# Layer 2 into its feed-forward: norms of three batches as pieces of the attention, a fixed TensorE order up to the gathers, and layer 3's first keys loaded in two column parts

## The chip, the cores and the metric

The kernel runs on one core of a Trainium2 chip. The metric is the device time of one execution in microseconds; the number given for a kernel is the median of its runs. The engines are called PE (TensorE), DVE (VectorE), ACT (ScalarE), POOL (GpSimd) and SP (SyncE, which here issues DMAs).

## What is computed

Four layers run in one program over x of 4 batches x 256 tokens x 256 features, each as a norm, a cross attention to a context (4 x 1601 x 256) and a residual addition, then a norm, a feed-forward and a residual addition. The change lies at the end of layer 2's attention, in layer 2's feed-forward, and in the loads that open layer 3:

```python
x = x + _L2_xattn_ref(_layernorm(x, axis=-1), ctx_2048, ...)
x = x + _L2_ffn_ref(_layernorm(x, axis=-1), L2_ffn_Wr, L2_ffn_br, L2_ffn_Wg, L2_ffn_Wu, L2_ffn_Wd)
x = x + _L3_xattn_ref(_layernorm(x, axis=-1), ctx_2048, ...)

def _layernorm(x, axis=-1, eps=1e-05):
    m = jnp.mean(x, axis=axis, keepdims=True)
    v = jnp.var(x, axis=axis, keepdims=True)
    return (x - m) / jnp.sqrt(v + eps)

def _L2_ffn_ref(hidden_states, Wr, br, Wg, Wu, Wd):   # 4 experts, 1024 hidden units each, best one per token
    logits = x @ Wr + br
    probs = jax.nn.softmax(logits, axis=-1)
    top_w, top_idx = jax.lax.top_k(probs, 1)
    g = jnp.einsum('td,edf->tef', x, Wg); u = jnp.einsum('td,edf->tef', x, Wu)
    y = jnp.einsum('tef,efd->ted', jax.nn.silu(g) * u, Wd)
    ...
```

## The kernel before

The layers follow each other in one instruction stream per engine. A scheduler places the instructions of each engine, by their dependences and its own costs; an instruction given to `self.pin` keeps its place in the program's order relative to other pinned ones on its engine. While `self.strict` is true, `self.mm` and `self.ordered` pin every matmul that goes through them. In the kernel before, `strict` is false in layer 2's feed-forward. Register loads (`value_load`) are not pinned by it.

**Layer 2's attention** (`l2_xattn`) goes through units of one batch and one group of four heads, `units = [(b, g) ...]`, with four groups per batch. The loop over heads and column pairs (`step` 0 to 7) interleaves the scores of one head with the softmax, the turns of the probabilities (`pT`, DVE, L1613) and the value products of the head before; `pieces` prepares the next unit, and `project` multiplies by `wo` and adds to x (`acc`, L1635). The last unit's tail follows the loop.

**Layer 2's feed-forward** (`l2_ffn`) first takes the norm of each batch (`layernorm`, L1033: statistics on DVE, the root as a Sqrt activation on ACT in `rstd`, L125, which needs its own activation table, then a reciprocal and `f2xn` on DVE, L160), writes `f2xd` to memory, transposes on PE (`tp_ln`, L1040) into `f2xT`, with the copy by ACT (L114) or DVE (L112) in turn, and multiplies by the router (`f2lg`, 8 x 2 products of 4 columns). Batches 0 to 2 have their final x long before the attention's end, and the scheduler moves their statistics and Sqrt there, while the writing of `f2xn` stays behind the attention. From the logits DVE and ACT work out softmax, gate and one-hot choice `oh`; `f2ct` (two PE products) counts tokens per expert; DVE works out the place of each token (`te` to `cols`, L1077 to L1113) and the expert of each of the 11 token blocks (`ei`, L1128). `f2st` (8 products of `rows` and `cols`) gives `src`, by which POOL gathers the blocks (`f2xr`, L1134). Each block is transposed (`brought`, `f2tpx`, L1148), its expert's number is loaded into a register of each engine that uses it (L1150), and `gated`, `turned` and `down` go over 4 chunks x 11 blocks, with `load(c)` fetching the weights of a chunk.

**Fills.** `fill(n)` takes n steps of `l3_early`, layer 3's key and value products of batch 0 (`f2fill`, one step: a key product of `ctxK`, its copy by ACT, a value product of `ctxT`, its copy by ACT, L1787, and sums of squares, L1909 and L1912). They keep PE at work while the router's decisions are made. The counts are 1 and 3 around the router, 2 after `ct`, 2 after the gathers, then one per loop turn for five turns.

**Layer 3's opening** (`l3_open`) runs after the attention: it makes `idb` and sets the ones in `va3` (L1735, L1754, L1755, all on DVE) and loads `wkv`, the whole `ctxK` and `ctxT` of batch 0, and `wq`, on SP's queue. All SP loads keep the program's order.

Of the kernel before, what the change touches and what calls it, by code (L numbers as in the profile page):

```python
# [24 lines left out]
P = 128  # L25
B = 4
# [71 lines left out]
class Kernel:  # L98
# [69 lines left out]
    def wide_take(self):  # L168
# [3 lines left out]
        return self.psf[n].tile([P, 512], F32, name=name, tag=tag)  # L172

# [814 lines left out]
    def l2_ffn(self, other):  # L988
# [13 lines left out]
        with ExitStack() as es:  # L1002
# [6 lines left out]
            xd = self.dram.tile([NT, D], F32, name="f2xd")  # L1009
# [17 lines left out]
            with tc.tile_pool(name="f2r", bufs=1) as rt:  # L1027
                low, keep, lane, tok, order = self.low, self.keep[:, :E2], self.lane, self.tok, self.order

                xn = rt.tile([P, 8, D], F32, name="f2xn")  # L1030
                xT = rt.tile([P, 2, NT], F32, name="f2xT")
                for b in range(B):
                    self.layernorm(xn[:, 2 * b : 2 * b + 2, :], self.x[b])  # L1033
                    nc.scalar.dma_start(
                        xd.rearrange("(t p) d -> p t d", p=P)[:, 2 * b : 2 * b + 2, :], xn[:, 2 * b : 2 * b + 2, :]
                    )
                    tp = ps.tile([P, 2, 2, P], F32, name="tp_ln", tag="tp")
                    for k in range(2):
                        for q in range(2):
                            nc.tensor.transpose(tp[:, k, q, :], xn[:, 2 * b + q, k * P : (k + 1) * P], self.ident)  # L1040
                    self.evac(xT[:, :, b * S : (b + 1) * S], tp.rearrange("p k q t -> p k (q t)"))
                    if b == 2:
                        chunks.append(load(0))
                        fill(1)
                lgt = ps_g.tile([P, 512], F32, name="f2lg", tag="gu")
                lg = lgt[:, : 8 * E2].rearrange("p (t e) -> p t e", e=E2)
                for t in range(8):
                    for k in range(2):
                        self.mm(lg[:, t, :], xT[:, k, t * P : (t + 1) * P], wr[:, k, :], k == 0, k == 1)
                fill(3)  # L1050
# [6 lines left out]
                nc.scalar.activation(l, l, AF.Exp)  # L1057
                pr = rt.tile([P, 8, E2], F32, name="l2_pr")
# [15 lines left out]
                fill(2)  # L1074
# [54 lines left out]
                nc.vector.tensor_copy(slot, sf)  # L1129

# [9 lines left out]
            fill(2)  # L1140
            expert = []
# [219 lines left out]
    def l2_xattn(self):  # L1361
# [10 lines left out]
        with ExitStack() as es:  # L1372
# [297 lines left out]
            self.es2.close()  # L1670
            main = es.enter_context(tc.tile_pool(name="a2main", bufs=2, side="right", reuse_waits="tile"))


# [3 lines left out]
            for n, (b, g) in enumerate(units):  # L1677
# [5 lines left out]
                for h in range(4):  # L1683
                    hd = {"ms": self.small.tile([P, 2, 8], F32, name="nmsm2"), "p": [], "va": va, "at": at, "h": h, "b": b,
                          "wo": wo_now}
                    for c in (0, 2):
# [18 lines left out]
                        if pieces is not None:  # L1705
                            for _ in range(WHEN[step]):
                                next(pieces, None)
# [780 lines left out]
```

## Time and profile before

| | |
|---|---|
| runs | 2398.01, 2399.74, 2392.47, 2402.09 us; median 2398.87 us |
| the profiled execution | 2395.95 us, its span 2394.2 us |
| granted clock of TensorE, mean | 0.97 |
| PE busy | 2260.8 us, 94% of the span |
| DVE, ACT, POOL busy | 62%, 53%, 40% of the span |
| layer 2's attention, one unit with a norm's table loads, one without | 61.96 us, 61.96 us |
| attention's last product ends / router's last ends / `ct` / `st` / first `f2tpx` | 1693.32 / 1708.63 / 1717.24 / 1723.20 / 1728.71 us |

A row of the timeline reads: start, busy time, engine, line, operation, tile written and tiles read, shape, count, and in brackets the idle time before it on its engine with what ended it. In a table of stretches each row is a stretch of the span with the busy time of each engine in it, the granted TensorE clock (PEclk, 1.00 is full), the DMA engines' share and their GB/s. PEld is TensorE's weight load, PEldq an instruction of TensorE's own sequencer.

### The profile page before, as it was taken

The page shows a single profiled execution, that of the slowest core. Times are in us where ns is not written, and L with a number is a line of the kernel's source. Part 1 is how long each engine was busy: PE and PEld are TensorE (multiplying, and loading weights), DVE is VectorE, ACT ScalarE, POOL GpSimd, SP SyncE. Part 2 cuts the span into 40 slices and gives each one's busy share as a digit, 9 for nine tenths or more (in the row PEclk, how much of TensorE's full clock was granted, in tenths as well). Part 3 has the DMA queues.
Part 4 walks back from the last instruction along what each step waited for, and adds up shares of the span by engine and source line. Part 5 has one row for each costly group of instructions (what it writes and reads, how often), then busy time and mean ns, then how long its engine had stood idle before and what let it go on. Part 6 is the DMA issues. An engine that isn't in the chain of part 4 may idle for free.

```text
span 2394.2 us, 42217 instructions
## 1 busy us (share of the span) xinstructions
PE 2260.8 (94%) x14322; PEld 1385.9 (58%) x14335; DVE 1474.3 (62%) x3553; ACT 1271.3 (53%) x2877; POOL 945.7 (40%) x1707
## 2 busy tenths in 40 slices
PE   8989997889989999999999999999899889999996
PEld 5777875777845555555555555555665533444332
DVE  5453532674457777877777777777334474758344
ACT  3334443452464555555555555553232477888994
POOL 1014654512335444555554555554121253334220
PEclk9989998989999999999999999999899989999998
DMA  7165575662550111111111111100534364434320
GB/s 266 41 201 163 169 149 147 205 191 60 165 184 25 50 51 43 51 51 51 51 51 51 51 51 51 45 7 10 204 126 115 88 166 118 105 97 101 84 61 22
DMA packets 156078, 234.47 MB, mean 98 GB/s; under 512 B 33929, under 2 KB 122761, under 8 KB 154666
## 3 DMA queue, kind: packets, MB, share of 16 engines
q1 hardware_dynamic: 138998, 190.07, 25.7%
q0 software_dynamic: 11280, 31.60, 5.6%
q10 hardware_dynamic: 5588, 10.09, 1.4%
q8 instruction: 117, 1.92, 0.3%
q14 instruction: 95, 0.78, 0.1%
HBM read 169.94 MB, written 61.74 MB: 97 GB/s over the span
## 4 chain that ended last, share of the span: by engine, by line
PE 81%; DVE 7%; issue 4%; DMA 3%; ACT 2%; POOL 2%; SPq 1%; ACTq 0%; another core or an unknown queue 0%; POOLq 0%; DVEq 0%
PE o L117 17%; PE s L117 17%; PE o L77 7%; PE b L77 3%; PE f2gu L117 3%; PE s L77 3%; PE fill L1307 3%; PE f1gu L117 2%; PE acc L117 2%; PE f0gu L117 2%; PE tpq L117 2%; PE av L117 2%; PE f0y L117 2%; PE f2y L117 1%; PE f1y L117 1%
## 5 line engine op out<-in xcount | busy, mean ns | idle before, releaser
L1572 ACT ACTIVATE p<-s,nmsm 128x448 f32<-128x448 f32 (+2 forms) x512 | 324.2, 638 | 369.8 <-DVE nmsm L1567 313.4
L117 PE MATMUL o<-pT,va 128*128 128x256 f32 (+2 forms) x1920 | 431.8, 377 | 3.0 <-DVE pT L1613 2.8
L117 PE MATMUL s<-kT,qT 128*32 128x448 f32 (+2 forms) x4096 | 424.2, 550 | 4.2 <-ACT p L1572 4.2
L77 ACT ACTIVATE e<-s 128x1024 f32<-128x1024 f32 (+1 forms) x416 | 392.2, 1041 | 57.3 <-PE s L77 56.1
L117 PEld LDWEIGHTS o<-pT,va 128*128 128x128 f32 (+1 forms) x1920 | 344.8, 190 | 127.5 <-issue 75.4
L1607 POOL TENSOR_SCALAR p<-p,rm 128x448 f32<-128x448 f32 (+2 forms) x512 | 319.4, 645 | 6.3
L1567 DVE TENSOR_REDUCE nmsm<-s 128x1 f32<-128x448 f32 (+4 forms) x384 | 293.4, 784 | 4.4
L1613 DVE STREAM_TRANSPOSE pT<-p 128x448 f32<-128x448 f32 (+4 forms) x384 | 278.1, 779 | 10.7 <-POOL p L1607 10.7
L117 PEld LDWEIGHTS s<-kT,qT 128*32 128x32 f32 x4096 | 121.7, 110 | 250.2 <-issue 213.8
L77 PE MATMUL o<-e,va 128*32 128x512 f32 x1656 | 248.8, 618 | 12.5 <-DVE os L77 10.7
L1600 POOL TENSOR_TENSOR rm<-em,tot 32x8 f32<-32x8 f32 x256 | 49.9, 195 | 336.2 <-DVE tot L1597 303.8
L1564 DVE TENSOR_TENSOR s<-s,mask 128x64 f32<-128x64 f32 (+4 forms) x384 | 92.6, 260 | 128.6 <-PE s L117 82.5
L77 PEld LDWEIGHTS s<-qb,kb 32*128 32x128 f32 (+1 forms) x1664 | 65.4, 181 | 183.6 <-issue 148.5
L1307 PE MATMUL fill<-wkc_early,ctxT 128*128 128x256 f32 (+1 forms) x444 | 110.5, 401 | 9.0 <-ACT va_early L1315 6.8
L522 POOL DMA_INDIRECT f0xr<-f0xd,f0src x95 | 90.7, 955 | 68.8 <-PE f0gu L117 16.9
L77 PE MATMUL s<-qb,kb 32*128 32x256 f32 (+1 forms) x1664 | 111.4, 331 | 2.9 <-ACT e L77 1.8
L77 POOL CAST kb<-kf 128x384 fp32r<-128x384 f32 (+1 forms) x126 | 65.1, 545 | 101.6 <-PE s L77 47.9
L1307 PEld LDWEIGHTS fill<-wkc_early,ctxT 128*128 128x128 f32 (+1 forms) x444 | 87.1, 200 | 25.3 <-ACT va_early L1315 7.9
L1572 ACT ACTIVATION_READ_ACCUMULATOR p<-s,nmsm 128x1 f32 x512 | 100.5, 196 | 0.0
L1326 DVE TENSOR_REDUCE ss_early<-sq_early 128x4 f32<-128x512 f32 x64 | 37.1, 580 | 84.4 <-ACT sq_early L1325 62.9
L630 POOL DMA_INDIRECT f0yt<-f0yd,f0slot x64 | 62.9, 983 | 62.4 <-DVE x L622 30.7
L117 PE MATMUL f2gu<-f2wgu,f2xsT 128*128 x176 | 84.4, 604 | 0.8 <-issue 0.5
(579 smaller groups left out, 3698.5 us busy)
## 6 DMA issues: line engine op xcount, KB each, us to landing
kf<-kd SPq DMA_DIRECT2D x384, 48.0 KB
vd<-va_early SPq DMA_DIRECT2D x96, 128.0 KB
kd<-kT_early SPq DMA_DIRECT2D x48, 256.0 KB
kT<-kd SPq DMA_DIRECT2D x16, 768.0 KB
va<-vd SPq DMA_DIRECT2D x16, 768.0 KB
kd<-kt SPq DMA_DIRECT2D x96, 128.0 KB
f0yd<-f0ys SPq DMA_DIRECT2D x95, 128.0 KB
ctxT<-in_ctxT SPq DMA_DIRECT2D x5, 1664.0 KB
```

The source lines that it names most:

```text
L77: ins = f(*a, **kw)
L117: self.ordered(self.nc.tensor.matmul(out, lhsT, rhs, start=start, stop=stop, **kw))
L522: nc.gpsimd.indirect_dma_start(out=t, out_offset=None, in_=xd[:, :], in_offset=bass.IndirectOffsetOnAxis(ap=src[:, n : n + 1], axis=0),)
L630: nc.gpsimd.indirect_dma_start(out=yt, out_offset=None, in_=yd[:, :], in_offset=bass.IndirectOffsetOnAxis(ap=slot[:, t, r : r + 1], axis=0),)
L1307: ins = nc.tensor.matmul(tp[:rows, t, :], ctxT[u // NKV2][:, k, c0 : c0 + rows], w[u % NKV2][:, k, :], start=k == 0, stop=k == 1,)
L1326: nc.vector.tensor_reduce(ss[:, m0:m1], sq[:, : m1 - m0, :], AX.X, ALU.add)
L1564: nc.vector.tensor_tensor(sv, sv, mask[:, e0:e1, : nt - CT, :].rearrange("p n t i -> p n (t i)"), ALU.add)
L1567: nc.vector.tensor_reduce(ms[:, 0, e0:e1], s[:, n0:n1, : nt * 32], AX.X, ALU.max, negate=True)
L1572: nc.scalar.activation(p[:, n, : nt * 32], s[:, n, : nt * 32], AF.Exp, bias=ms[:, 0, e : e + 1], accum_out=ms[:, 1, e : e + 1],)
L1600: nc.gpsimd.tensor_tensor(r[32 * a : 32 * a + 32], e[:, a], tot, ALU.mult)
L1607: nc.gpsimd.tensor_scalar(p[:, n, : nt * 32], p[:, n, : nt * 32], r[:, e : e + 1], 1.0, ALU.mult, ALU.mult)
L1613: self.pin(nc.vector.transpose(pT[:, 2 * c + n0 : 2 * c + n1, :nt, :].rearrange("p n t i -> p n (t i)"), p[:, n0:n1, : nt * 32],))
```

## The change

Four edits, all between layer 2's attention and layer 3:

1. The norms of batches 0, 1 and 2 are made inside the attention. `settled(b)` is a generator of four pieces (statistics; the root by `root`, a Newton iteration of twelve DVE operations without ACT; the two `f2xn`; the write of `f2xd` on SP's queue), taken at steps 0 and 7 of the units g = 1 and g = 2 of the next batch. Batch 3 keeps `layernorm` in the feed-forward.
2. In `l2_ffn`, `strict` is true from the start until the gathers and `fill(2)` are issued. Per batch: four transposes, the copy (ACT; DVE for batch 3), eight router products. The fills before the first expert are 2 after the router, 3 after `ct`, 2 after the gathers. Activation tables are loaded ahead by a one-column activation, `table`: Sqrt in the attention's tail, Exp after the last norm, Silu after Exp.
3. In `l3_open` the context comes in two column parts, 0 to 512 and 512 to the end, with the feed-forward's first weights between them.
4. The cast of `idb` and the memsets of `va3` go from DVE to POOL.

```diff
--- before.py
+++ after.py
@@ -170,6 +170,10 @@
         self.flip4 = (self.flip4 + 1) % 4
         n, name, tag = ((0, "fill", "tpf"), (2, "filly", "y"), (1, "fillg", "gu"), (0, "fillt", "tp"))[self.flip4]
         return self.psf[n].tile([P, 512], F32, name=name, tag=tag)
+
+    def table(self, of):
+
+        self.pin(self.nc.scalar.activation(self.small.tile([P, 1], F32, name="one2"), self.eps6, of))
 
     def fill(self, n):
 
@@ -1006,7 +1010,7 @@
             ps = es.enter_context(tc.tile_pool(name="f2ps", bufs=2, space=PSUM))
             ps_g = es.enter_context(tc.tile_pool(name="f2pg", bufs=2, space=PSUM))
             ps_y = es.enter_context(tc.tile_pool(name="f2py", bufs=2, space=PSUM))
-            xd = self.dram.tile([NT, D], F32, name="f2xd")
+            xd = self.xd2
             yd = self.dram.tile([NS * P, D], F32, name="f2yd")
 
             def load(c):
@@ -1027,27 +1031,34 @@
             with tc.tile_pool(name="f2r", bufs=1) as rt:
                 low, keep, lane, tok, order = self.low, self.keep[:, :E2], self.lane, self.tok, self.order
 
-                xn = rt.tile([P, 8, D], F32, name="f2xn")
+                chunks.append(load(0))
+                self.strict = True
+                for _ in self.loads3:
+                    pass
                 xT = rt.tile([P, 2, NT], F32, name="f2xT")
+                lgt = ps_g.tile([P, 512], F32, name="f2lg", tag="gu")
+                lg = lgt[:, : 8 * E2].rearrange("p (t e) -> p t e", e=E2)
                 for b in range(B):
-                    self.layernorm(xn[:, 2 * b : 2 * b + 2, :], self.x[b])
-                    nc.scalar.dma_start(
-                        xd.rearrange("(t p) d -> p t d", p=P)[:, 2 * b : 2 * b + 2, :], xn[:, 2 * b : 2 * b + 2, :]
-                    )
+                    if b < B - 1:
+                        xn = self.xn2[:, 2 * b : 2 * b + 2, :]
+                    else:
+                        xn = rt.tile([P, 2, D], F32, name="f2xn3")
+                        self.layernorm(xn, self.x[b])
+                        self.table(AF.Exp)
+                        nc.scalar.dma_start(xd.rearrange("(b q p) d -> b p q d", p=P, q=2)[b], xn)
                     tp = ps.tile([P, 2, 2, P], F32, name="tp_ln", tag="tp")
                     for k in range(2):
                         for q in range(2):
-                            nc.tensor.transpose(tp[:, k, q, :], xn[:, 2 * b + q, k * P : (k + 1) * P], self.ident)
-                    self.evac(xT[:, :, b * S : (b + 1) * S], tp.rearrange("p k q t -> p k (q t)"))
-                    if b == 2:
-                        chunks.append(load(0))
-                        fill(1)
-                lgt = ps_g.tile([P, 512], F32, name="f2lg", tag="gu")
-                lg = lgt[:, : 8 * E2].rearrange("p (t e) -> p t e", e=E2)
-                for t in range(8):
-                    for k in range(2):
-                        self.mm(lg[:, t, :], xT[:, k, t * P : (t + 1) * P], wr[:, k, :], k == 0, k == 1)
-                fill(3)
+                            self.ordered(
+                                nc.tensor.transpose(tp[:, k, q, :], xn[:, q, k * P : (k + 1) * P], self.ident)
+                            )
+                    (nc.vector.tensor_copy if b == B - 1 else nc.scalar.copy)(
+                        xT[:, :, b * S : (b + 1) * S], tp.rearrange("p k q t -> p k (q t)")
+                    )
+                    for t in range(2 * b, 2 * b + 2):
+                        for k in range(2):
+                            self.mm(lg[:, t, :], xT[:, k, t * P : (t + 1) * P], wr[:, k, :], k == 0, k == 1)
+                fill(2)
                 wide = lambda ap: ap[:, :, None].to_broadcast([P, 8, E2])
                 l = rt.tile([P, 8, E2], F32, name="l2_l")
                 nc.vector.tensor_tensor(l, lg, rb[:, None, :].to_broadcast([P, 8, E2]), ALU.add)
@@ -1055,6 +1066,7 @@
                 nc.vector.tensor_reduce(mx, l, AX.X, ALU.max)
                 nc.vector.tensor_tensor(l, l, wide(mx), ALU.subtract)
                 nc.scalar.activation(l, l, AF.Exp)
+                self.table(AF.Silu)
                 pr = rt.tile([P, 8, E2], F32, name="l2_pr")
                 self.share(rt, "l2", pr, l)
 
@@ -1071,7 +1083,7 @@
                 ohm = oh.rearrange("p t e -> p (t e)")
                 self.mm(pre, low, ohm, True, True)
                 self.mm(tot, self.ones, ohm, True, True)
-                fill(2)
+                fill(3)
                 by_e = lambda ap: ap.rearrange("p (t e) -> p e t", e=E2)
                 te = rt.tile([P, E2, 8], F32, name="f2te")
                 nc.vector.tensor_copy(te, by_e(tot))
@@ -1127,6 +1139,7 @@
                 nc.vector.tensor_reduce(ef, ge, AX.X, ALU.add)
                 nc.vector.tensor_copy(ei, ef)
                 nc.vector.tensor_copy(slot, sf)
+            self.es4.close()
 
             xr = []
             for n in range(NS):
@@ -1138,6 +1151,7 @@
                 xr.append(t)
             chunks.append(load(1))
             fill(2)
+            self.strict = False
             expert = []
             xsT = one.tile([P, NS, 2, P], F32, name="f2xsT")
             acc = [one.tile([P, D], F32, name=f"f2acc{n}") for n in range(NS)]
@@ -1668,8 +1682,31 @@
             for _ in self.early:
                 pass
             self.es2.close()
+            self.xn2 = self.es4.enter_context(tc.tile_pool(name="pre2", bufs=1, side="right")).tile(
+                [P, 2 * (B - 1), D], F32, name="f2xn"
+            )
+            self.xd2 = self.dram.tile([NT, D], F32, name="f2xd")
             main = es.enter_context(tc.tile_pool(name="a2main", bufs=2, side="right", reuse_waits="tile"))
 
+
+            def settled(b):
+
+                mv = self.small.tile([P, 2, 2], F32, name="mv2")
+                for q in range(2):
+                    st = self.small.tile([P, 6], F32, name="st3")
+                    nc.vector.bn_stats(st, self.x[b][:, q, :])
+                    nc.vector.bn_aggr(mv[:, q, :], st)
+                yield
+                r = self.small.tile([P, 8], F32, name="r2_8")
+                self.root(r[:, :2], mv[:, :, 1], 1.0, 1e-5, r[:, 2:])
+                yield
+                xn = self.xn2[:, 2 * b : 2 * b + 2, :]
+                for q in range(2):
+                    nc.vector.tensor_scalar(
+                        xn[:, q, :], self.x[b][:, q, :], mv[:, q, 0:1], r[:, q : q + 1], ALU.subtract, ALU.mult
+                    )
+                yield
+                nc.sync.dma_start(self.xd2.rearrange("(b q p) d -> b p q d", p=P, q=2)[b], xn)
 
             WHEN = [0, 1, 1, 1, 1, 1, 1, 0]
             BETWEEN = [0, 0, 0, 0, 0, 0, 1, 0]
@@ -1705,6 +1742,10 @@
                         if pieces is not None:
                             for _ in range(WHEN[step]):
                                 next(pieces, None)
+                        if step in (0, 7) and b and g in (1, 2):
+                            if (g, step) == (1, 0):
+                                norm = settled(b - 1)
+                            next(norm, None)
                         if step == 7 and last is not None:
                             project(last)
                         if soft is not None and c == 0:
@@ -1718,6 +1759,7 @@
                 next(soft[0])
                 next(vals)
                 if n == 0:
+                    self.table(AF.Sqrt)
                     next(soft[0])
             for _ in value_steps(hd):
                 pass
@@ -1732,13 +1774,23 @@
         self.idb = self.a3.tile([P, P], BF16, name="idb")
         self.mv3 = self.a3.tile([P, B, 2, 2], F32, name="mv3")
         self.rs3 = self.a3.tile([P, B, 2], F32, name="rs3")
-        nc.vector.tensor_copy(self.idb, self.ident)
+        nc.gpsimd.tensor_copy(self.idb, self.ident)
         self.va3 = [self.values3(self.a3)]
         self.wkv3 = self.a3.tile([P, 2, 512], F32, name="wkv3")
-        nc.sync.dma_start(self.wkv3, i["l3_wkv"].rearrange("(k p) e -> p k e", p=P))
-        self.ctx3 = [self.load_ctx3(n, 0) for n in range(2)]
         self.wq3 = self.a3.tile([P, 2, D], F32, name="wq3")
-        nc.sync.dma_start(self.wq3, i["l3_wq"].rearrange("(k p) e -> p k e", p=P))
+        self.ctx3 = [self.a3.tile([P, 2, MP], F32, name=f"ctx3{n}") for n in range(2)]
+
+        def loads():
+            self.pin(nc.sync.dma_start(self.wkv3, i["l3_wkv"].rearrange("(k p) e -> p k e", p=P)))
+            for cols in (slice(0, 4 * P), slice(4 * P, MP)):
+                for n in range(2):
+                    v = i[("ctxK", "ctxT")[n]][0].rearrange("(k p) m -> p k m", p=P)
+                    self.pin(nc.sync.dma_start(self.ctx3[n][:, :, cols], v[:, :, cols]))
+                yield
+            self.pin(nc.sync.dma_start(self.wq3, i["l3_wq"].rearrange("(k p) e -> p k e", p=P)))
+
+        self.loads3 = loads()
+        next(self.loads3)
 
     def load_ctx3(self, n, b):
         t = self.a3.tile([P, 2, MP], F32, name=f"ctx3{n}")
@@ -1751,8 +1803,8 @@
         n = 16 * (HD3 + 1)
         for h in range(2):
             t = va[:, :, h, :]
-            self.nc.vector.memset(t[:, :, :n].rearrange("p m (h e) -> p m h e", e=HD3 + 1)[:, :, :, HD3:], 1.0)
-            self.nc.vector.memset(t[:, :, n:], 1.0)
+            self.nc.gpsimd.memset(t[:, :, :n].rearrange("p m (h e) -> p m h e", e=HD3 + 1)[:, :, :, HD3:], 1.0)
+            self.nc.gpsimd.memset(t[:, :, n:], 1.0)
         return va
 
     def l3_begin(self, b, st):
@@ -2337,6 +2389,7 @@
         self.swb = self.const.tile([P, 1], F32, name="swb")
         self.csum = self.const.tile([P, 2, B], F32, name="csum")
         self.es2 = ExitStack()
+        self.es4 = ExitStack()
         self.e2 = self.es2.enter_context(tc.tile_pool(name="e2", bufs=1, side="right"))
         self.sort_tables()
         self.l0_xattn()
```

## The prediction

> **What bounds the kernel now.** I read the page first, for the engine that sets the span:
>
> ```profile
> span 2394.2 us, 42217 instructions
> PE 2260.8 (94%) x14322; PEld 1385.9 (58%) x14335; DVE 1474.3 (62%) x3553; ACT 1271.3 (53%) x2877; POOL 945.7 (40%) x1707
> PE 81%; DVE 7%; issue 4%; DMA 3%; ACT 2%; POOL 2%; SPq 1%; ACTq 0%; another core or an unknown queue 0%; POOLq 0%; DVEq 0%
> ```
>
> TensorE is busy 94% of the span and 81% of the chain that ended last. So an edit pays only where TensorE idles, runs at the half clock, or waits in its own instruction stream. Next, busy time by stretches: first two units of layer 2's attention (the second holds the hoisted norm with its table loads), then the opening of the feed-forward, cut at the ends of its steps and at the clock's changes.
>
> ```profile
> core 0: us, PE busy (x) PEld busy (x) DVE busy (x) ACT busy (x) POOL busy (x), PEclk, DMA share, GB/s
> 906.48:968.44 61.96, 61.95 (x419) 36.29 (x419) 47.87 (x103) 31.84 (x90) 31.95 (x71) 1.00 0.15 49
> 968.44:1030.40 61.96, 61.95 (x419) 36.29 (x419) 49.01 (x108) 34.58 (x92) 31.95 (x71) 1.00 0.15 49
> ...
> 1693.31:1696.75 3.44, 1.03 (x7) 0.74 (x7) 3.05 (x11) 0.21 (x1) 0.00 (x0) 1.00 0.58 183
> 1696.75:1700.17 3.42, 3.42 (x18) 3.24 (x17) 2.00 (x8) 2.19 (x3) 0.00 (x0) 0.50 1.02 426
> 1717.24:1723.20 5.96, 5.79 (x30) 4.81 (x28) 5.26 (x26) 2.89 (x8) 0.00 (x0) 1.00 0.92 383
> 1728.71:1734.45 5.74, 4.47 (x9) 1.99 (x10) 0.42 (x1) 1.66 (x2) 2.37 (x3) 0.70 0.32 88
> ```
>
> Both attention units last 61.96 us with TensorE busy 61.95, though the second holds 2.74 us more of ScalarE. The window from 1693.31 is mostly idle, and the five after it (to 1713.82) have PEclk 0.50. Third, TensorE's rows in that opening:
>
> ```profile
> 1692.29 1.03 PE L117 MATMUL acc<-wo,at 128*128 128x256 f32 x4
> 1695.72 2.57 PE L1040 MATMUL tp_ln<-ident,f2xn 128*128 128x128 f32 x12 [2.41 <-DVE f2xn L160]
> 1698.08 5.12 PE L117 MATMUL f2lg<-r,f2xT 128*128 128x4 f32 x24
> 1706.76 1.87 PE L117 MATMUL f2lg<-r,f2xT 128*128 128x4 f32 x8 [0.79 <-DVE f2xT L112]
> 1717.24 0.30 PE L117 MATMUL f2ct<-f2oh,low 128*128 128x32 f32 x2
> 1717.61 5.43 PE L117 MATMUL f2fill<-wkv,ctx 128*128 128x256 f32 x24
> 1723.20 1.95 PE L117 MATMUL f2st<-f2cols,f2rows 128*128 128x11 f32 x16 [0.17 <-DVE f2cols L1113]
> 1728.71 0.41 PE L1148 MATMUL f2tpx<-ident,f2xr 128*128 128x128 f32 x2 [1.73 <-DMA f2xr<-f2xd,f2src]
> ```
>
> The attention's last product ends at 1693.32, the router at 1708.63; ct runs at 1717.24, st at 1723.20, the first token transposes at 1728.71, and the first expert's f2gu ends at 1734.45. Last, the line that reads the expert numbers into TensorE's registers:
>
> ```profile
> L1150 PEldq TENSOR_LOAD <-f2ei x11: 294/301/311, 1725.0 to 1758.0; - x11
> L1150 PEldq FUSED_REGOPS  x11: 146/151/151, 1725.4 to 1758.4; - x11
> L1150 PEldq EVENT_SEMAPHORE  x10: 51/51/51, 1723.9 to 1724.9; - x10
> ```
>
> Eleven loads, spread over 33 us: two before the first tokens, the others one per loop turn of 3.02 us, where TensorE stays 99% busy, so they are free. Two in a row are 0.69 us apart (1724.97, 1725.67), and the ten semaphore events took 1.06 us.
>
> **Norms as pieces in the attention.** Six table loads of 1.28 us leave ScalarE, but a unit with two of them takes the same 61.96 us as one without: worth 0. VectorE gets, per batch, twelve small operations instead of one reciprocal (12 x 0.19 = 2.3) and two xn (0.85, elsewhere 0.74): 3.1 us in a unit where it has 13 free. The cover is short in places: the last pT turn at a head's change ends 1.4 us before its product. If a piece falls there, TensorE waits for up to its length, about 1 us per boundary. Bounds 0 and +3; the row of free time is the nearer one, so +1. A gain is excluded, since TensorE is busy 61.95 of the 61.96 us.
>
> **Attention's end to the router's end (15.3 us now).** xn of batches 0 to 2 stands ready, so the 2.41 us wait for f2xn goes (the idb cast and four memsets went before it on VectorE, and now lie on the idle POOL). In its place comes a strict chain per batch: four transposes, ScalarE's copy, eight router products. Full clock: transposes 4 x 0.43, copies 3 x 0.58 + 0.69, router 4 x 0.98 (eight st records: 1.95 / 2), eight hand-offs at about 0.14: 9.2 us. Half clock: 4 x 0.86, 2.43, 4 x 1.87, 1.1: 14.4. The clock decides. In the rows it changes on a grid of 3.413 us and stays down while router products fill a window (1700.17 to 1703.58 was fully busy, mostly router, and 0.50 went on). So a fall 2 to 6 us in is likely: 11.2 to 13.1, taken 12.1, which is 3.2 less than now (bounds 6.1 and 0.9 less).
>
> **Router's end to ct (8.6 us).** VectorE's and ScalarE's softmax chain (4.2 us, of it 1.6 a key norm L1912 in between) is hidden by two fill products of each kind, m0 and m1. Under the strict order each value product waits for ScalarE's copy of its key product (0.37 and hand-offs: 0.6 us), the first also behind the preloaded Silu table, 1.28. At full clock a product (eight records of fill, 5.43 / 3) is 1.81 for k and v, so 6.4; at half 9.0. The clock rises only after a busy window: taken 8.3, a gain of 0.3 (2.2 to -0.4).
>
> **ct to st (5.96 us): the dear one.** The changed order of instructions puts all eleven register loads between ct and st, because the order is held for matmuls but these loads are free to move up: one after m3's key product, seven after its value product, three after m4's key product. They are issued by TensorE's own sequencer, and st, the gather behind it and every fill stand after them. Eleven x 0.69 + 1.06 = 8.7 us, beside 5.4 us of fills. What the queue ahead covers is one product (0.9) each time: 7 x 0.69 - 0.9 = 3.95 idle, 3 x 0.69 - 0.9 = 1.2 idle. Fills 5.4, those, 0.6 + 0.2 of copy waits, and the rest of the first load: 12.3 us at full clock, 16.3 at half. An idle stretch of 4 us can bring the half clock back: the window from 1693.31, with 1.03 us busy, did. Taken 14.3: +8.3 (6.3 to 10.3). VectorE's cols are ready 5.9 after ct and no longer decide.
>
> By the Trainium skill ("TensorE: Matmul & The Clock Gate", Part 1 and "Why this matters for your kernels") one idle window of some 3 us halves the rate, and gaps above that are to be avoided. That rule speaks against this change; by it alone the stretch would be the half-clock one. Its Part 4 says that transposes don't count as busy; the trace partly disagrees: 188.06 to 191.47 was 92% busy, mostly with transposes, and kept its full clock.
>
> **st to the first tokens (5.51).** Two memsets on POOL now stand between st and the first gather (VectorE's took 0.23 and 0.21; POOL's 128x128 0.21, so about 0.5, of which the src cast hides half), and the fills may run at half clock: 6.1, +0.6 (0 to 1.5). **Tokens to the first expert's end (5.74).** f2gu took 3.65 at half clock where 1.72 is usual; with Silu's table in place and more fills ahead the clock is likelier to be up: 4.0, -1.7 (-2.7 to -0.5). **After it** one more product lies in the loop, since seven instead of eight run before the first expert: +1.8. Leaving the loop saves the register loads nothing. Keys in two parts: all 10 MB still land by about 25 us after the attention, and the first fill at 1703.06 stood behind router products, not behind its keys; 0. The new f2xd writes on SP's queue stand behind an attention that reads them 100 us later: 0.
>
> **Sum.** 1 - 3.2 - 0.3 + 8.3 + 0.6 - 1.7 + 1.8 = +6.5 us. The profiled execution took 2395.95 us (span 2394.2 and 1.75 around it), 2.9 under the median 2398.87 of the runs; so 2402.5 for it, and 2405.4 on the median. About 0.3% (7.2 us) is what a measurement of this kernel can tell from no change, and the sum lies just inside. With the router's stretch at 11.2 to 13.1, ct to st 2 us either way and the attention at 0 to 3, its own range is +2 to +11.
>
> **The rivals.** *The loads run beside the matmuls.* For it: in the loop they cost nothing. Against: there one load stands per 14 matmul rows, here seven in a row. ct to st then stays near 6 to 7.5, the clock isn't lost there, and the sum is -1 to -9.2 (full clock throughout: 9.2 + 6.4 + 6 + 5.5 + 3.0 = 30.1 against 41.1, and 1.8 back): 2390 to 2398. It is measurably faster only if the clock holds too. *Half clock to the first expert.* The fall comes in the first window, and router products, then load gaps, keep every window from lifting it: 14.4 + 9.0 + 16.3 + 7.0 + 5.2 = 51.9 against 41.1, + 1.8 + 1: +13.6, 2412.5. It decides once no window between the router and st is over some 80% busy, as those that lifted the clock in the rows were. *Nothing that is moved was on the path*: norms free, loads half covered, gains equal losses: 2399.
>
> **How the numbers follow.** The forecast 0.50 (of it 0.27 over 7.2 us), loads beside the matmuls 0.23 (0.20 measurably faster), half clock throughout 0.17, nothing moved 0.10. Faster 0.20, same 0.23 + 0.03 + 0.10 = 0.36, slower 0.27 + 0.17 = 0.44. The range 2390 to 2412 takes in the first rival and all but the end of the second.
>
> **What would show it.** Right: L1150's loads all between ct and st, with TensorE idle about 5 us among them; ct nearer the attention's end by 3 to 4 us, st further by 3 to 6; attention units of 61.96 still. Wrong: ct to st under 8 us, PEclk at 1.00 through the router, or units of 63 us, each of which ends one step above.

## The result, and the profile after

The changed kernel takes 2401.79 us (median of 41 runs, 2393.32 to 2407.36), the kernel before 2396.45 us (median of 67): ratio 1.0022, 95% interval 1.0016 to 1.0028, that is 5.3 us slower (3.8 to 6.7). That is below 0.3%, though the many runs set it apart from no change. The change's profiled run has a span of 2397.6 us, against 2394.2.

TensorE's rows through the stage after the change (start, busy time, engine, line, operation, tiles, shape, count, and in brackets the idle time before it with its releaser):

```profile
1688.12 3.05 PE L117 MATMUL acc<-wo,at 128*128 128x256 f32 x12
1691.01 0.60 PE L1053 MATMUL tp_ln<-ident,f2xn 128*128 128x128 f32 x4
...
1699.94 1.87 PE L117 MATMUL f2lg<-r,f2xT 128*128 128x4 f32 x8 [0.79 <-DVE f2xT L1055]
...
1709.44 0.30 PE L117 MATMUL f2ct<-f2oh,low 128*128 128x32 f32 x2
...
1713.83 1.13 PE L117 MATMUL f2fill<-wkv,ctx 128*128 128x256 f32 x4 [0.46 <-ACT kr L1839]
1718.92 2.04 PE L117 MATMUL f2fill<-wkv,ctx 128*128 128x256 f32 x4 [3.96 <-issue]
1721.43 2.08 PE L117 MATMUL f2fill<-wkv,ctx 128*128 128x256 f32 x4 [0.46 <-ACT kr L1839]
1723.30 3.43 PE L117 MATMUL f2st<-f2cols,f2rows 128*128 128x11 f32 x16
...
1732.06 0.38 PE L1162 MATMUL f2tpx<-ident,f2xr 128*128 128x128 f32 x2
```

The 2.41 us wait after the attention is gone, and `ct` comes 18.3 us after the end of the attention's last product (1691.17) where it came 23.9 us after it. Then, between a fill and the next one, stand 3.96 us of idle time that no semaphore ends ("issue"), and `st` starts 13.9 us after `ct` instead of 6.0. The register loads, by the line that makes them, lie around that gap:

```profile
L1164 PEldq TENSOR_LOAD <-f2ei x11: 296/299/310, 1712.5 to 1720.3; - x11
L1164 PEldq EVENT_SEMAPHORE  x10: 51/51/51, 1711.4 to 1712.4; - x10
```

All eleven start between 1712.5 and 1720.3, seven of them in a row from 1713.84 to 1717.96, where before they went from 1725.0 to 1758.0. The table of stretches shows what followed from it:

```profile
core 0: us, PE busy (x) PEld busy (x) DVE busy (x) ACT busy (x) POOL busy (x), PEclk, DMA share, GB/s
966.30:1028.26 61.96, 61.93 (x420) 36.27 (x419) 50.92 (x121) 31.87 (x90) 32.02 (x71) 1.00 0.17 54
...
1714.96:1718.92 3.96, 0.00 (x1) 0.03 (x1) 0.39 (x2) 0.37 (x1) 0.00 (x0) 0.86 0.95 397
1718.92:1723.30 4.38, 3.92 (x9) 2.66 (x10) 0.00 (x0) 0.37 (x1) 0.00 (x0) 0.50 0.02 7
1723.30:1732.06 8.76, 8.30 (x30) 6.82 (x28) 0.86 (x2) 1.75 (x4) 4.22 (x7) 0.54 0.11 33
1732.06:1735.55 3.49, 3.25 (x13) 1.90 (x12) 0.00 (x0) 1.02 (x3) 0.95 (x1) 1.00 0.22 67
```

TensorE does nothing for 3.96 us, and the granted clock falls to 0.50 inside that gap (at 1717.78) and stays there until 1731.43, just before the first tokens: `st` takes 3.43 us where it took 1.95. VectorE and ScalarE are nearly idle in it too (0.39 and 0.37 us), and no semaphore ends it. That points to the queue of TensorE's own sequencer; e1 and e6 below test it. The attention unit that holds pieces of a norm has VectorE busy 50.92 us instead of 49.01, and still lasts 61.96 us. The chain of waits names the same gap:

```profile
1713.83 1.14 PE f2fill L117 x4
1714.98 3.94 issue
1718.92 2.06 PE f2fill L117 x4
```

From here on a **stage time** is used: from the start of VectorE's last addition of the attention (`x<-x,acc`) to the start of its last `f2acc` in the feed-forward, within one profile. It is 177.5 us before and 182.7 us after, +5.2, close to the 5.3 us between the medians. (The two profiled spans differ by 3.4 us only, since the changed kernel's profile reaches the stage 2.1 us earlier.)

### The profile page after: what moved, and what is told of

It is laid out like the page before. It is cut to its first block, busy times and chain, and to the rows that moved or that the text cites. A ratio compares the mean times of both kernels' runs of the same rounds, so it can differ in the third digit from the quotient of the medians.

```text
span 2397.6 us, 42252 instructions
## 1 busy us (share of the span) xinstructions
PE 2259.9 (94%) x14322; PEld 1384.7 (58%) x14335; DVE 1477.9 (62%) x3576; ACT 1267.0 (53%) x2872; POOL 950.8 (40%) x1716
## 4 chain that ended last, share of the span: by engine, by line
PE 80%; DVE 8%; issue 5%; ACT 3%; DMA 3%; POOL 2%; another core or an unknown queue 0%; ACTq 0%; POOLq 0%; DVEq 0%; SPq 0%
PE o L117 17%; PE s L117 16%; PE o L77 7%; PE b L77 4%; PE s L77 3%; PE f2gu L117 3%; PE f1gu L117 2%; PE fill L1321 2%; PE acc L117 2%; PE tpq L117 2%; PE f0gu L117 2%; PE av L117 2%; PE f0y L117 2%; PE s L322 2%; DMA f0xr<-f0xd,f0src 1%
## 5 line engine op out<-in xcount | busy, mean ns | idle before, releaser
L1627 DVE STREAM_TRANSPOSE pT<-p 128x448 f32<-128x448 f32 (+4 forms) x384 | 278.2, 779 | 11.3 <-POOL p L1621 11.2
L77 PE MATMUL o<-e,va 128*32 128x512 f32 x1656 | 248.0, 616 | 13.9 <-DVE os L77 11.8
L77 PEld LDWEIGHTS s<-qb,kb 32*128 32x128 f32 (+1 forms) x1664 | 66.0, 181 | 182.7 <-issue 142.8
L1321 PEld LDWEIGHTS fill<-wkc_early,ctxT 128*128 128x128 f32 (+1 forms) x444 | 86.5, 199 | 25.2 <-ACT va_early L1329 8.0
L634 POOL DMA_INDIRECT f0yt<-f0yd,f0slot x64 | 62.7, 979 | 62.4 <-DVE x L626 30.5
L77 PEld LDWEIGHTS o<-e,va 128*32 128x32 f32 x1656 | 40.8, 109 | 76.3 <-issue 37.2
```

What stands on the lines that cost most here:

```text
L77: ins = f(*a, **kw)
L634: nc.gpsimd.indirect_dma_start(out=yt, out_offset=None, in_=yd[:, :], in_offset=bass.IndirectOffsetOnAxis(ap=slot[:, t, r : r + 1], axis=0),)
L1321: ins = nc.tensor.matmul(tp[:rows, t, :], ctxT[u // NKV2][:, k, c0 : c0 + rows], w[u % NKV2][:, k, :], start=k == 0, stop=k == 1,)
L1627: self.pin(nc.vector.transpose(pT[:, 2 * c + n0 : 2 * c + n1, :nt, :].rearrange("p n t i -> p n (t i)"), p[:, n0:n1, : nt * 32],))
```

## The experiments

My theory was that the register loads, bunched between `ct` and `st`, cost what they take in the sequencer, plus the clock. The rivals: the loads lie beside other work; the copy waits and the clock under the strict order carry the loss; VectorE's new work or the keys' loads do.

The sets of runs below have a kernel before of 2343.86, 2340.04 and 2342.29 us (median of each set), some 55 us under the first measurement, so only ratios within a set and stage times are compared. Most of the difference lies ahead of the change: the changed kernel's second profile is 7.9 us ahead of its first at 372 us, 43.9 at 468 and 48.8 at 742. Stage times come from one profile per run. The ratio is the one on record for each run; the quotient of the two medians differs from it by up to 0.0007. By the ratio alone e1, e6, e14 and e7 can't be told from the kernel before.

| run | stage, us | router's end / `te` / `src` / first silu, us from the stage's start | ratio to before, 95% interval |
|---|---|---|---|
| before | 177.5 | 15.3 / 24.5 / 31.8 / 41.1 | |
| after | 182.7 | 10.6 / 18.8 / 35.6 / 44.4 | 1.0022 (1.0016 to 1.0028) |
| r1, the changed kernel again | 182.9 | 12.3 / 21.4 / 36.1 / 44.5 | 1.0030 (1.0019 to 1.0041) |
| e1, loads behind `st` | 173.9 | 10.6 / 18.8 / 27.9 / 35.6 | 0.9995 (0.9983 to 1.0007) |
| e3, not strict | 175.1 | 8.6 / 12.9 / 20.2 / 36.8 | 0.9989 (0.9978 to 1.0000) |
| e6, keys in one part | 176.4 | 12.1 / 21.4 / 30.5 / 38.0 | 0.9995 (0.9984 to 1.0007) |
| e14, e1 and keys in one part | 175.3 | 11.7 / 20.0 / 29.2 / 36.9 | 1.0002 (0.9993 to 1.0012) |
| e7, norms alone | 177.8 | 14.4 / 24.6 / 32.0 / 41.4 | 0.9997 (0.9985 to 1.0008) |
| e4, strict order alone | 185.2 | 18.9 / 31.5 / 39.7 / 48.6 | 1.0029 (1.0014 to 1.0044) |
| e9, e1 and products first | 174.0 | 12.1 / 18.7 / 25.9 / 34.3 | 0.9978 (0.9966 to 0.9991) |
| e16, router free, loads late | 174.5 | 7.3 / 14.0 / 23.8 / 35.0 | 0.9987 (0.9976 to 0.9998) |
| e21, all of it | 171.7 | 8.4 / 15.0 / 22.3 / 34.7 | 0.9974 (0.9962 to 0.9986) |

The four marks are the starts of `l_l` (VectorE's first reading of the router), `te` (its first reading of `ct`), `src`, and of the first `f2h`.

**r1, the changed kernel again.** Its bracket is the same 3.96 us, though the router part ended 1.7 us later:

> The changed kernel itself, so that it stands on the same chip as the others of this set. Theory: the stretch from the attention's end to the last f2acc 182.7 us as in its first profile, the eleven register loads between ct and st, ratio to before 1.002 (1.0016 to 1.0028 in the first measurement).

```profile
1672.31 1.64 PE L117 MATMUL f2fill<-wkv,ctx 128*128 128x256 f32 x4 [3.96 <-issue]
```

**e1: the loads behind `st`.**

```diff
-                nc.vector.tensor_copy(ei, ef)
+                nc.vector.scalar_tensor_tensor(ei, st[:1, :NS], 0.0, ef, ALU.mult, ALU.add)
```

> The changed kernel with one edit: the expert numbers ei are written by one VectorE operation that also reads st, so that no register load can stand before st; the loads then lie one per loop turn again (the two memsets ahead of the first gather move behind the third gather with it). Theory, the register loads between ct and st cost what they take in TensorE's sequencer: ct to st falls from 13.9 us to 6 to 8, the 3.96 us of idle and the half clock after it go, st to the first expert's end falls from 12.2 to 9 to 11, together 8 to 11 us less than the changed kernel, so 2391 to 2394 where the kernel before has 2396.5 (ratio to before 0.998). Rival, the half clock and the waits for ScalarE's copies under the strict order carry the loss and the loads only fill time that is idle anyway: 0 to 3 us less than the changed kernel, ratio 1.001 to 1.002.

```profile
1661.28 0.30 PE L117 MATMUL f2ct<-f2oh,low 128*128 128x32 f32 x2
...
1669.10 1.85 PE L117 MATMUL f2st<-f2cols,f2rows 128*128 128x11 f32 x16
...
1674.96 0.41 PE L1162 MATMUL f2tpx<-ident,f2xr 128*128 128x128 f32 x2 [0.60 <-DMA f2xr<-f2xd,f2src]
```

```profile
L1164 PEldq TENSOR_LOAD <-f2ei x11: 297/300/309, 1671.5 to 1702.4; - x11
```

`ct` to `st` is 7.8 us, `st` takes 1.85, the first tokens come 5.9 us after it: the stage is 8.8 us shorter, inside what the theory asked for and far from the rival's 0 to 3. Everything up to `te` is the same to 0.04 us in both profiles (10.6, 18.8), and the matmuls stand in the same order up to the first silu, so the difference is the loads and what they pull along. One thing more moved: POOL's two memsets, ahead of the first gather in the changed kernel, stand behind the third here; e6 below, where they stay, shows nearly the same gain. By the ratio the expected 2391 to 2394, which are 2.5 to 5.5 us under before, weren't shown: 0.9995 is 1.2 us under before, in an interval from 4.0 under to 1.6 over. Against the changed kernel's second measurement (1.0030) it is 0.0035, or 8 us, and the two intervals don't meet.

**e3: no strict order.** All else as in the changed kernel.

```diff
                 chunks.append(load(0))
-                self.strict = True
```

> The changed kernel with the strict order left off, all else kept: matmuls are placed by the scheduler, key and value products pair up without waits for ScalarE's copies, and all eleven register loads stand together right after st, in the time of the gathers. Theory, the loads cost their issue time wherever they stand together on the way to the first expert: ct to st falls to about 6 us (8 less), st to the first tokens grows from 8.8 to some 11 to 13 (8.7 us of loads ahead of the fills and the transposes), so 3 to 6 us less than the changed kernel, ratio to before 1.000 to 1.001. Rival, loads behind st are covered by the wait for the gathers: 7 to 10 us less, ratio 0.998 to 0.999.

```profile
L1163 PEldq TENSOR_LOAD <-f2ei x11: 294/299/307, 1666.8 to 1673.8; - x11
1665.63 1.85 PE L117 MATMUL f2st<-f2cols,f2rows 128*128 128x11 f32 x16
1674.57 6.15 PE L117 MATMUL f2fill<-wkv,ctx 128*128 128x256 f32 x20 [7.09 <-issue]
```

The eleven loads stand in one block behind `st` (1666.8 to 1673.8), and TensorE idles 7.09 us on them, in the time of the gathers. The gain on the changed kernel, 7.6 us of stage, is the rival's number, but not for its reason: the loads were not covered (`src` to the first silu took 16.6 us; 9.3 before), and it is the front that came 5.9 us earlier at `te`, because the transposes begin among the attention's last products and no value product waits for a copy ahead of `st`. So in the changed kernel the strict order costs some 5.9 us up to `te`, by one profile, which is not much less than the loads cost where they stand. `st` to the first tokens took 14.9 us, more than the theory's 11 to 13.

**e7: the norms alone, in the kernel before.** The pieces of the attention, and `l2_ffn` taking their xn for batches 0 to 2 (shown in part):

```diff
-                xn = rt.tile([P, 8, D], F32, name="f2xn")
                 for b in range(B):
-                    self.layernorm(xn[:, 2 * b : 2 * b + 2, :], self.x[b])
+                    if b < B - 1:
+                        xn = self.xn2[:, 2 * b : 2 * b + 2, :]
+                    else:
+                        xn = rt.tile([P, 2, D], F32, name="f2xn3")
+                        self.layernorm(xn, self.x[b])
```

> The kernel before with the pieces of the norms alone: xn of batches 0 to 2 is made inside layer 2's attention, the rest (no strict order, fills 1, 3, 2, 2, keys in one part, memsets on VectorE) stays. Theory: attention units keep 61.96 us, the 2.41 us wait for f2xn after the attention goes and the transposes and router products follow at once, so 2 to 4 us less than before, ratio 0.9985 to 0.999. Rival, the added VectorE work holds the turns of the probabilities: units of 62.5 to 63 us and no gain, ratio 1.000 to 1.001.

```profile
1646.12 2.98 PE L117 MATMUL f2lg<-r,f2xT 128*128 128x4 f32 x16 [0.20 <-DVE f2xT L112]
1652.35 2.05 PE L117 MATMUL f2fill<-wkv,ctx 128*128 128x256 f32 x4 [3.26 <-DMA ctx<-in_ctxK]
1654.19 1.06 PE L1041 MATMUL tp_ln<-ident,f2xn 128*128 128x128 f32 x4
```

The rival's longer units didn't come, and of the theory the gain didn't. The wait for xn goes, three batches of router products are done 5.6 us after the attention, and a new wait stands there: a fill that the scheduler put ahead of the last batch's transposes needs the keys, whose whole 1.7 MB land at 8.8 us. The attention itself is untouched: over its 14 additions to x from 809 to 1616 us the profile moves by 0.28 us against the kernel before, and r1, with the same pieces, by -0.03; so VectorE's new work costs 0.3 us at most in all.

**e4: the strict order alone, in the kernel before.**

```diff
                 xn = rt.tile([P, 8, D], F32, name="f2xn")
+                self.strict = True
 ...
             fill(2)
+            self.strict = False
             expert = []
```

> The kernel before with the strict order alone (from the norms to the fills behind the gathers); norms, fills 1, 3, 2, 2, keys and memsets as before. In its order two register loads stand before st and two between st and the first tokens. Theory, the strict order costs a wait of 0.46 us for ScalarE's copy per product pair and what the two loads take (2 x 0.69 + 1.06), part of it under the wait for the gathers: stretch to the last f2acc 179 to 182 us where before has 177.5, ratio 1.001 to 1.002. Rival, an order held in place brings the products nearer together and the clock up: 175 to 177, ratio 0.999.

```profile
1650.11 2.56 PE L1041 MATMUL tp_ln<-ident,f2xn 128*128 128x128 f32 x12 [2.41 <-DVE f2xn L160]
1657.04 2.04 PE L117 MATMUL f2fill<-wkv,ctx 128*128 128x256 f32 x4 [4.36 <-DMA ctx<-in_ctxK]
1659.73 6.83 PE L117 MATMUL f2lg<-r,f2xT 128*128 128x4 f32 x32
1670.91 3.78 PE L117 MATMUL f2fill<-wkv,ctx 128*128 128x256 f32 x8 [0.74 <-ACT kr L1789]
```

Worse than either idea, 7.7 us of stage. The held order puts one fill between batch 2 and batch 3, and TensorE waits 4.36 us for the keys there, with all router products behind that fill. That is 3.5 us at the router's end. Another 3.5 are added between there and `te`, where value products wait for ScalarE's copies and the clock stays at 0.50 until 27.6 us after the stage's start (20.5 in the kernel before).

**e6 and e14: the keys in one part**, in the changed kernel and in e1.

```diff
-            for cols in (slice(0, 4 * P), slice(4 * P, MP)):
+            for cols in (slice(0, MP),):
```

> The changed kernel with layer 3's first context loaded in one column part, ahead of the feed-forward's first weights. Theory, the first fill stands behind the router and not behind its keys: as the changed kernel within 1 us, ratio to before 1.002. Rival, the fills now wait for the whole of the keys, 1.7 MB each: the first fills start 2 to 4 us later and the time grows by as much, ratio 1.003 to 1.004.

> The kernel with ei behind st (e1) and, in addition, the keys in one column part. Its order of instructions on TensorE is that of e1. Theory, the column parts are covered while the router ends 10.6 us after the attention: whole keys land at 8.8 us (the wait in the run with the norms alone ended there), so the stretch to the last f2acc is 173.9 us as in e1, within 1 us, ratio to before as e1's (0.9995). Rival: the first value product waits for its keys, 2 to 4 us more, ratio 1.001.

```profile
L1164 PEldq TENSOR_LOAD <-f2ei x11: 297/299/313, 1671.3 to 1709.2; - x11
1676.14 1.85 PE L117 MATMUL f2st<-f2cols,f2rows 128*128 128x11 f32 x16
```

e6 says little about the keys: with two transfers fewer the scheduler placed the register loads anew, from 1671.3 to 1709.2 with `st` at 1676.14, three of them ahead of `st`, while the matmuls kept the changed kernel's order up to the first silu. `ct` to `st` is 7.8 us, as in e1, and from `l_l` to the first silu it is 25.9 us where the changed kernel took 33.7. So e6 is a second test of the bunch, with another edit and the memsets left ahead of the gathers, and it agrees with e1. It also says that the bunching is an accident of this order. e14 holds TensorE's order as in e1 and so separates the keys: its 1.3 us over e1 are there at the router's end (11.7 against 10.6), ahead of any fill, and from `l_l` to the first silu the two agree (25.2 and 25.0). By these two profiles the column parts are worth nothing in the changed kernel, as long as its first fill stands 10 us behind the attention.

**e9: e1, and both products of a fill ahead of its copies.** The products in the loop stay (its head becomes `for n in range(2):`), the copies follow it:

```diff
-                copy(out, ps if n == 0 else ps.rearrange("p (g h d) -> p g h d", g=2, d=HD3))
+            copy(st["kr"][:, m, :], tile[:, :D])
+            copy(self.l3_value(va, m), tile[:, D:].rearrange("p (g h d) -> p g h d", g=2, d=HD3))
```

> The kernel with ei behind st (e1) and, in addition, both products of a fill ahead of its two copies; the strict order from the norms on stays. Theory, each wait of 0.46 us for ScalarE's copy (five of them ahead of st and two behind it) and the 0.85 us behind the Silu table go: the stretch to the last f2acc is 3 to 4 us less than the 173.9 of e1, 170 to 171, ratio 0.997 to 0.998. Rival, the waits only move: cols, not the fills, then decide st, and the gathers the first tokens, so that 1 us or less is left: 173, ratio 0.999.

```profile
1669.33 1.95 PE L117 MATMUL f2st<-f2cols,f2rows 128*128 128x11 f32 x16
1671.14 3.70 PE L117 MATMUL f2fill<-wkv,ctx 128*128 128x256 f32 x16
1675.58 0.41 PE L1162 MATMUL f2tpx<-ident,f2xr 128*128 128x128 f32 x2 [0.74 <-ACT va L1840]
1677.65 1.96 PE L117 MATMUL f2gu<-f2wgu,f2xsT 128*128 x4 [1.66 <-DMA f2xr<-f2xd,f2src]
```

The copy waits among the fills are gone (3.15 us of them in e1), and part comes back: 0.74 and 1.66 us of waiting at the first tokens. From `l_l` to the first silu it is 22.2 us against 25.0. The stage, 174.0, hides that, since the router took 1.5 us longer here than in e1 and the loop behind the first silu 1.4 us longer (139.8 against 138.4; why isn't known). So the stage is not the theory's 170 to 171 but near the rival's 173, while the ratio, 0.9978, is the theory's number; its interval takes in both.

**e16: the router free, the loads late, products first.** Strict from `ct` on, with the edits of e1 and e9.

> The changed kernel with three edits: the strict order starts only at ct, so that the transposes and router products may move into the attention's tail; ei reads st, so that the register loads stay behind it; and each fill makes both its products before its two copies, so that no value product waits for ScalarE's copy of the key product. Theory, the three costs add up: router end 8.6 us after the attention (10.6 in the changed kernel), ct at 12.8 (18.6), st at 18.2 (32.2), first expert's silu at 27 to 29 (44.4), stretch to the last f2acc 166 to 168 us (182.7; 177.5 before), so 9 to 11 us under the kernel before, ratio 0.995 to 0.996. Rival, the second column parts of the keys, queued behind 3.1 MB of expert weights, land too late for m4 (the first load of the stage is issued at the attention's end and 5.9 MB lie before them): TensorE waits 2 to 4 us, ratio 0.997.

```profile
1659.94 1.10 PE L117 MATMUL f2fill<-wkv,ctx 128*128 128x256 f32 x4 [0.36 <-DMA ctx<-in_ctxK]
1662.75 1.13 PE L117 MATMUL f2fill<-wkv,ctx 128*128 128x256 f32 x4 [1.71 <-DMA ctx<-in_ctxT]
1663.71 2.18 PE L117 MATMUL f2st<-f2cols,f2rows 128*128 128x11 f32 x16
...
1672.22 0.41 PE L1162 MATMUL f2tpx<-ident,f2xr 128*128 128x128 f32 x2 [1.43 <-DMA f2xr<-f2xd,f2src]
1674.30 2.77 PE L117 MATMUL f2gu<-f2wgu,f2xsT 128*128 x4 [1.67 <-PEq L1164]
```

The rival's wait came: once the front is quick, the second column parts, queued behind 3.1 MB of expert weights, are 2.1 us late and hold `st`. That is only part of what is missing from 166 to 168: from `st` to the first silu it took 13.4 us where 9 to 11 were expected, with waits for the gather and for register loads (`PEq`, TensorE's sequencer) at the first tokens.

**e21: what the runs point to.** e16 with the second column parts ahead of `load(0)`, `fill(3)` behind the gathers, and the first block's expert number in a tile of its own that doesn't read `st`:

```diff
+                nc.vector.tensor_copy(ei0, ef[:, :1])
 ...
-                expert.append(nc.tensor.value_load(ei[:, n : n + 1], min_val=0, max_val=E2 - 1))
+                e = ei[:, n : n + 1] if n else ei0
+                expert.append(nc.tensor.value_load(e, min_val=0, max_val=E2 - 1))
```

> The version that the runs point to: the changed kernel with the router free to move into the attention's tail (strict from ct on), both products of a fill ahead of its copies, the keys' second column parts ahead of the expert weights (in the run without that they came 2.1 us late), the first block's expert number read alone ahead of st and the other ten behind it, and three fills instead of two behind the gathers, so that the first tokens wait for neither fills nor loads. Theory: ct at 13 us after the attention, st at 18.3 to 18.6, the first tokens at 26, first silu at 29 to 31, the stretch to the last f2acc 166 to 168 us (182.7 in the changed kernel, 177.5 before): ratio 0.995 to 0.996. Rival, the gap at the gathers and the clock take the gain back as in the run before (174.5 there): 172 to 175, ratio 0.998 to 0.999.

```profile
1657.80 5.62 PE L117 MATMUL f2fill<-wkv,ctx 128*128 128x256 f32 x24
1663.26 1.95 PE L117 MATMUL f2st<-f2cols,f2rows 128*128 128x11 f32 x16
1665.07 5.43 PE L117 MATMUL f2fill<-wkv,ctx 128*128 128x256 f32 x24
1672.20 0.42 PE L1164 MATMUL f2tpx<-ident,f2xr 128*128 128x128 f32 x2 [1.71 <-DMA f2xr<-f2xd,f2src]
```

```profile
core 0: us, PE busy (x) PEld busy (x) DVE busy (x) ACT busy (x) POOL busy (x), PEclk, DMA share, GB/s
1666.00:1669.00 3.00, 3.00 (x15) 2.65 (x14) 0.69 (x1) 1.37 (x4) 2.12 (x3) 1.00 0.91 380
```

The shortest stage, 5.8 us under before and 11 under the changed kernel, and the lowest ratio, 0.9974, though its interval overlaps those of e9 and e16. It missed 166 to 168 and lies just under the rival's 172 to 175: `st` came 1.7 us or more later than expected, the first tokens 3.2, the first silu 3.7 or more. The gathers are one reason: the first tokens come 7.0 us after `src` where they came 3.5 after it in the kernel before. The stretch from 1666.00 to 1669.00 has the DMA engines 0.91 busy, since weights are still under way that early, and the first gather took 5.8 us from issue to landing, where e6 and r1, with the DMA engines nearly free at that point, show 2.8 and 2.9. That contention holds the gather is an inference from these numbers; it wasn't tried by itself.

## Why the prediction was right

The forecast was 2405.4 us, +6.5; measured 2401.79, +5.3. (The forecast stood on a median of four runs, 2398.87; on the median of 67, 2396.45, the same +6.5 makes 2402.95.) The direction and mechanism were those of the trace. Step by step, with the profile's own stretches:

- *Attention, +1 (0 to +3).* Near 0: units of 61.96 us, and 0.3 us over 14 additions. The lower end was right; a piece at the short cover of a head's change did not show.
- *Router, 12.1.* 10.6 in one profile, 12.3 in the other, from the same instructions. The granted clock fell at 1697.30 in the first, 6.1 us after the attention's end, and 3.4 us after it in the second, whose longer router is the same fall met earlier. The estimated range (11.2 to 13.1) was right in kind; its lower end was 0.6 us too high.
- *Router to `ct`, 8.3.* 7.6, and 8.5 in r1.
- *`ct` to `st`, 14.3.* 13.9, and 13.4 in r1; the idle time worked out for the seven loads, 3.95 us (7 x 0.69 - 0.9 is 3.93), is 3.96 in the profile, and 3.96 again in r1. The 1.2 us set down for the three loads behind them did not show: the row at 1721.43 waits 0.46 us, for a copy, and the product ahead of them took 2.04 us at the half clock instead of 0.9. e1 and e6 showed that the loads are the cause of the long stretch.
- *`st` to first tokens, 6.1.* 8.8, the one term outside its bounds: its upper end was 7.0. In r1 it is 6.8. I had priced the clock in `ct` to `st`, but the fall hits hardest behind it, where PEclk is 0.54 and `st` itself takes 1.5 us more; the tokens stand behind two fills that are slowed as well. In r1 the clock was at 1.00 through `st`. POOL's two memsets took 0.47 and 0.31 us, overlapping, 0.62 in all against about 0.5 assumed, but the first tokens waited for no gather.
- *First expert, 4.0.* 3.5 in both. *The extra product in the loop, +1.8.* From the first silu to the last `f2acc` 138.4 against 136.3, +2.0.

Without the attention the terms make 5.5 where the stage shows 5.2. In the first profile that closeness is partly luck: the router was 1.5 us shorter than taken, router to `ct` 0.7 shorter, and `st` to the first tokens 2.7 longer. In r1, with the same stage time to 0.2 us, each term but the attention's 1 lies within 1 us of the forecast. The signs show the same: `ct` came 5.7 us nearer the attention's end and `st` 2.2 further, outside the 3 to 4 and 3 to 6 that were named, and in r1 3.1 and 4.4. The prediction's own range, +2 to +11, comes to +2.6 to +11.5 by its terms.

Of the rivals, "the loads beside the matmuls" fell with the 3.96 and 7.09 us of "issue"; "half clock to the first expert" is half true, since the clock rose ahead of `ct` (1707.54) and fell again in the gap; that the keys' parts move nothing is right for this kernel and wrong where a fill stands earlier (e16, e7). What the trace of before could not show is how much the strict order costs in the router part: e3 puts it at 5.9 us at `te`, and the kernel that frees the router, holds the loads back and brings the keys first, with three small edits more (e21), is under the kernel before.

On the rule of the Trainium skill ("TensorE: Matmul & The Clock Gate", "Why this matters for your kernels") that a gap of over some 3 us costs the rate: PEclk went from 1.00 to 0.50 inside the gap of 3.96 us in the first profile and 0.4 us behind the same gap in r1, which agrees. Shorter gaps were no protection here: at the attention's end the changed kernel lost the full clock with no gap above 0.72 us, and e3 lost it after a window of 3.41 us (1647.09 to 1650.50) in which TensorE was 0.92 busy, mostly with transposes and router products.

## What to carry to other kernels

An order that is held for matmuls alone leaves every unpinned instruction of that engine's queue free to move up, and register loads are issued in the same queue: list where they land before weighing a reordering. Here eleven of them close together, 8.7 us of issue by the prediction's count, cost 8.8 us of stage. Of that, 3.96 are idle in one piece; the rest I put down to the slower clock and to what lay behind. Spread out, they cost nothing that shows: three stand ahead of `st` in e6, whose `ct` to `st` is that of e1. A true dependence (an operand that isn't ready earlier) kept them in place in e1. And where the front of a stage is shortened, or a product moves up, ask at once which transfer it will now wait for: here it was the keys, three times (e7, e4, e16).

## What the runs showed of the hardware that I had not expected

- The same instructions of the router part took 10.6 or 12.3 us, and e1, e6, e9 and e14 fall between or on these (10.6, 12.1, 12.1, 11.7). The granted clock changes on a grid of 3.41 us (in the changed kernel at 1697.30, 1707.54, 1717.78 and 1731.43, 3, 3 and 4 steps apart), and it matters where the attention's end falls in it: the earlier the fall, the longer the router. It fell 6.1 us after that end in the two profiles with 10.6, 4.0 us after it with 11.7, 3.6 to 3.7 with 12.1, and 3.4 with 12.3. Differences below 2 us between two profiles of this stage are not to be read as an edit's.
- A memset on POOL took 0.48 and 0.32 us (128x208 and 128x182) where VectorE took 0.23 and 0.21.
